# An AdaLN block with attention and a mixture of experts on one core: the eight stores of a sequence's rows to the expert lists are planned one behind the other

## The chip, the cores and the metric

The kernel runs on one core of a Trainium2 chip. The metric is the device time of one execution in microseconds (us). A core has engines that work side by side, each through its own list of instructions in order: TensorE (PE in the profile, its weight loads PEld), VectorE (DVE), ScalarE (ACT), GpSimd (POOL) and SyncE (SP, which here only issues DMA transfers). An engine that has to wait for a semaphore holds up everything behind it in its list.

## The reference, cut to what matters

Eight sequences of 512 tokens with 256 features pass through one transformer block. Its first half is linear attention with a causal running sum, its second half a mixture of eight experts, of which each token uses two:

```python
h = _layernorm(x, axis=-1) * (1 + ca) + sa
x = x + ga * _L0_attn_ref(h, L0_attn_w_qkv, L0_attn_w_out)      # causal linear attention, 16 heads
h = _layernorm(x, axis=-1) * (1 + cb) + sb
x = x + gb * _L0_ffn_ref(h, L0_ffn_router_w, L0_ffn_w1, L0_ffn_w2)

# _L0_ffn_ref, for the tokens xf of all sequences
probs = jax.nn.softmax(xf @ router_w.T, axis=-1)
topv, topi = jax.lax.top_k(probs, 2)
topv = topv / (topv.sum(axis=-1, keepdims=True) + 1e-09)
cw = (jax.nn.one_hot(topi, e, dtype=xf.dtype) * topv[..., None]).sum(axis=1)
h = jax.nn.gelu(jnp.einsum('td,edh->teh', xf, w1), approximate=False)
y = jnp.einsum('teh,ehd->ted', h, w2)
out = jnp.einsum('te,ted->td', cw, y)
```

All of it is float32. The kernel computes only the two chosen experts of each token.

## The kernel before, in words

**Tiling.** A sequence is four chunks of 128 tokens, so there are 32 chunks. For each chunk `early` makes v, q and k (`v_ps`, `qk_ps`), `middle` the denominators and the transposed q and k (`cum_ps`, `qkT_ps`), `late` the scores, the running state and the output product (`s_ps`, `st_ps`, `oT_ps`, `a_ps`), and `rows_of` the second layer norm (`mv_f`, `scaled`, `row`, `rt_ps`).

**Lists of tokens.** After a sequence's fourth chunk, `route` picks two experts per token and a place in each expert's list (`slot`). The lists lie in device memory (`slots`). For each chunk and each of the two choices, POOL issues one indirect DMA that stores 128 rows of 521 numbers (0.27 MB) to their places: eight stores per sequence, 64 in all, line L1015. They are called scatters below. Two scatters of one sequence need not wait for each other: a place belongs to one pair of token and expert.

**Blocks of an expert.** `plan(b, ...)` decides after sequence b which blocks of an expert's list are full. `TAKE` fixes how many: one block of 128 rows after sequence 0, five after sequence 1, three after sequence 2, then two, two, two and four blocks of 256 rows after sequences 3 to 6. What is left is planned after sequence 7 (`plan_rest`, blocks named 8_0, 8_1 and so on). A block is fetched by SP (`fetch`: the weights w1 and w2 of 1 MB each, and the rows `sx` and `r` from the lists), turned by DVE (`xT`), multiplied by w1 and w2 on PE (`h_ps`, `y_ps`) with a Gelu on ACT between (`g`), scaled by DVE (`y`), and added to the result by an indirect DMA from POOL (line L1383). Blocks of sequence b may be read only when all scatters up to those of sequence b have landed.

**The order of the work.** Nothing here is issued as the Python loops run. Each piece of work is noted in a plan (`L.do`, `L.group`, `L.call`) with its engine, an estimate of its time, the tiles that it reads and writes, further works that it has to come behind (`after`), a level and, for a DMA, a landing time and its size. `Plan.run` then walks through time by these estimates: whenever an engine is free it gives it, of the works whose predecessors are done, the one with the lowest level. A DMA counts as done when it has landed: its issue, its `landing`, and its megabytes over a shared channel of 0.26 MB per us. The order that comes out is the fixed order of each engine's list. Attention of sequence b has levels from 4b, a sequence's scatters 4b + 3, expert matmuls 1000 and more, and the other work of blocks -50. So PE prefers attention and takes expert matmuls where no attention is ready. `after` is only an argument of this plan: the semaphores of the program are derived later from the tiles and the DMAs themselves, and `apart` declares that scatters need not wait for each other.

When two indirect DMAs come to stand next to each other on POOL, `give_out` puts a small memset (`between`, line L1519) between them.

Of the kernel before, what the change touches and what calls it, by code (L numbers as in the profile page):

```python
# [339 lines left out]
def kernel(  # L340
# [17 lines left out]
    NC = S // P  # L358
# [42 lines left out]
    scatters = []  # L401
# [532 lines left out]
    def route(q):  # L934
# [79 lines left out]
        def scatter(c, j):  # L1014
            s = nc.gpsimd.indirect_dma_start(  # L1015
                out=slots, out_offset=IndirectOffsetOnAxis(ap=slot.now()[:, c, j : j + 1], axis=0),
                in_=row.now()[:, c, :], in_offset=None,
                bounds_check=NONE - 1, oob_is_err=False,
            )
            apart(s, scattered + cleared, "a slot is of one pair of token and expert")  # L1020
            apart(s, gathered, "blocks that are read are full by then")
            scattered.append(s)
            return s

        L.level += LEVEL["scatter"]
        for c in range(NC):
            for j in range(2):
                scatters.append(
                    L.do(
                        "POOL", 1.29, lambda c=c, j=j: scatter(c, j), r=[slot, row], landing=2.0,  # L1030
                        mb=0.27,
                    )
                )
                scatters[-1].indirect = True
# [435 lines left out]
    for i in range(2):  # L1470
        for t, at in ((acc, TOK), (slots, NONE)):
            L.do(
                "SP", 0.5, lambda t=t, at=at, i=i: clear(t[at + i * P : at + (i + 1) * P, :]),
                after=[modded_], landing=3.0, mb=0.2,
            )
    seqs = {}
    for b in range(B):
        if b not in xs:
            L.level = 4 * b - 12
            load_x(b, after=[X.stores[b - XS]] if b >= XS else ())  # L1480
        L.level = 4 * b + LEVEL["open"]
        q = seqs[b] = open_(b, modded)
        for c in range(NC):
            for part, does in (("early", early), ("middle", middle), ("late", late)):
                L.level = 4 * b + c + LEVEL[part]
                does(q, c)
            L.level = 4 * b + c + LEVEL["rows"]
            rows_of(q, c, modded)

        def store(b=b, q=q):  # L1490
            s = nc.sync.dma_start(
                out=acc[ts(b, S), :].rearrange("(c p) d -> p c d", p=P), in_=q.x.now()
            )
            apart(s, added, "those are of earlier sequences")

        L.level = 4 * b + 3 + LEVEL["route"]
        X.stores.append(L.do("SP", 0.5, store, r=[q.x], landing=3.0, mb=0.5))
        route(q)
        if TAKE[b][0]:
            L.level = 4 * b + 3 + LEVEL["plan"]  # L1500
            blocks = plan(b, list(scatters))
            experts(blocks)
# [76 lines left out]
```

## Time and profile before

| what | us |
|---|---|
| median of 9 runs | 797.13 (794.43 to 798.04) |
| the profiled execution | 796.45 |
| its span from the first to the last instruction | 794.7 |
| PE busy in the span | 755.8 |
| DVE, POOL, ACT busy | 410.8, 319.7, 269.4 |
| the first two scatters start | 89.4 and 91.0 |
| the rows of the first block are fetched from | 111.9 |
| the first matmul of a block starts | 123.9 |
| the last scatter starts | 453.1 |
| the last matmul ends | 786.2 |

The span falls into three stages. Up to about 124 us there is attention only. Up to about 425 us attention and expert blocks share PE. From there to 786 us there are expert blocks only, and then the last sums are added. A group of the profile is named by what it writes and reads, so `h_ps<-xT,w` is the first product of a block. Nearly all operations of the compute engines are issued by one helper and so have line L221. PE's busy time counts a matmul from its start to a modelled end, so it doesn't show how densely the matmuls follow one another. A chunk gives four instructions `qk_ps` and four `a_ps`, and a block of 128 rows 16 `h_ps` and 16 `y_ps`.

### The profile page before, as it was taken

The page shows a single profiled execution, that of the slowest core. Times are in us where ns is not written, and L with a number is a line of the kernel's source. Part 1 is how long each engine was busy: PE and PEld are TensorE (multiplying, and loading weights), DVE is VectorE, ACT ScalarE, POOL GpSimd, SP SyncE. Part 2 cuts the span into 40 slices and gives each one's busy share as a digit, 9 for nine tenths or more (in the row PEclk, how much of TensorE's full clock was granted, in tenths as well). Part 3 has the DMA queues.
Part 4 walks back from the last instruction along what each step waited for, and adds up shares of the span by engine and source line. Part 5 has one row for each costly group of instructions (what it writes and reads, how often), then busy time and mean ns, then how long its engine had stood idle before and what let it go on. Part 6 is the DMA issues. An engine that isn't in the chain of part 4 may idle for free.

```text
span 794.7 us, 16196 instructions
## 1 busy us (share of the span) xinstructions
PE 755.8 (95%) x5824; PEld 620.6 (78%) x5824; DVE 410.8 (52%) x1379; ACT 269.4 (34%) x552; POOL 319.7 (40%) x480
## 2 busy tenths in 40 slices
PE   6799898899999999999999999999999999999995
PEld 2576667667777787778888888888988889888885
DVE  3989998999797866898754610111112111111110
ACT  4555344454634646636413111111111111111110
POOL 5844554726464273373542651312121232120332
PEclk9899999999999999999999999999999999999998
DMA  7322272976865396651666999776886978879961
GB/s 242 99 65 75 86 188 96 310 184 201 200 208 156 109 329 189 190 192 31 203 198 173 293 293 267 205 203 202 239 235 198 286 200 256 219 215 304 273 134 21
DMA packets 132131, 154.30 MB, mean 194 GB/s; under 512 B 43568, under 2 KB 115280, under 8 KB 131920
## 3 DMA queue, kind: packets, MB, share of 16 engines
q1 hardware_dynamic: 116640, 125.24, 52.7%
q0 software_dynamic: 15408, 28.00, 13.9%
q8 instruction: 47, 0.77, 0.4%
q14 instruction: 36, 0.29, 0.1%
HBM read 120.19 MB, written 37.20 MB: 198 GB/s over the span
## 4 chain that ended last, share of the span: by engine, by line
PE 46%; DMA 5%; issue 2%; POOL 1%; SPq 1%; DVE 0%; POOLq 0%
PE h_ps L221 21%; PE y_ps L221 21%; DMA out_dram<-y,to 4%; DMA out_dram<-acc 2%; POOL out_dram L1383 1%; PE oT_ps L221 1%; PE s_ps L221 1%; PE a_ps L221 1%; SPq L1366 1%; PE cum_ps L221 0%; PE rt_ps L221 0%; PE v_ps L221 0%; DVE row L221 0%; PE qk_ps L221 0%; PE qkT_ps L221 0%
## 5 line engine op out<-in xcount | busy, mean ns | idle before, releaser
L221 PE MATMUL h_ps<-xT,w 128*128 128x256 f32 (+1 forms) x1280 | 257.3, 348 | 3.7 <-DVE qk L221 2.7
L221 PE MATMUL y_ps<-w,g 128*128 128x256 f32 x1072 | 253.7, 380 | 0.3 <-issue 0.3
L221 PEld LDWEIGHTS h_ps<-xT,w 128*128 128x128 f32 x1280 | 214.6, 192 | 28.3 <-DVE qk L221 3.1
L221 PEld LDWEIGHTS y_ps<-w,g 128*128 128x128 f32 x1072 | 201.4, 190 | 27.7 <-issue 1.6
L221 ACT ACTIVATE g<-h_ps 128x512 f32<-128x512 f32 x134 | 80.0, 597 | 343.3 <-PE h_ps L221 343.1
L1383 POOL DMA_INDIRECT acc<-y,to x56 | 89.3, 1595 | 221.8 <-DVE y L221 189.5
L221 DVE SCALAR_TENSOR_TENSOR y<-y_ps,cw,r 128x256 f32<-128x256 f32 x67 | 30.0, 480 | 166.9 <-PE y_ps L221 166.8
L221 DVE TENSOR_TENSOR sm<-s_ps,causal 128x512 f32<-128x512 f32 x128 | 82.8, 680 | 9.9 <-PE s_ps L221 9.3
L221 DVE STREAM_TRANSPOSE xT<-sx 128x512 f32<-128x512 f32 (+1 forms) x40 | 24.9, 622 | 121.1 <-PE h_ps L221 69.3
L1015 POOL DMA_INDIRECT slots<-row,slot x64 | 64.6, 1009 | 32.8 <-issue 13.2
L221 POOL TENSOR_TENSOR f<-f,t 128x512 f32<-128x512 f32 x32 | 41.3, 1294 | 59.0 <-DVE t L221 21.0
L221 PE MATMUL qk_ps<-wqkv_sb,hT 128*128 128x512 f32 x128 | 62.2, 612 | 0.0
L221 ACT ACT_TABLE_LOAD x31 | 39.8, 1283 | 4.4 <-DMA cs<-in_cT_dram 3.1
L221 PEld LDWEIGHTS s_ps<-qT,kT 32*128 32x128 f32 x1024 | 32.3, 186 | 11.4 <-issue 8.2
L221 PE MATMUL oT_ps<-sm,vz 128*32 128x128 f32 x1024 | 39.8, 284 | 0.7 <-DVE sm L221 0.5
L1383 POOL DMA_INDIRECT out_dram<-y,to x11 | 17.1, 1555 | 56.4 <-DMA out_dram<-acc 23.1
L221 PE MATMUL s_ps<-qT,kT 32*128 32x128 f32 x1024 | 39.0, 284 | 0.1
L221 PEld LDWEIGHTS qk_ps<-wqkv_sb,hT 128*128 128x128 f32 x128 | 23.7, 195 | 19.0 <-issue 16.9
L221 PE MATMUL v_ps<-wqkv_sb,hT 128*128 128x256 f32 x128 | 35.4, 400 | 3.0 <-DVE t L221 1.9
L221 PE MATMUL a_ps<-wo,oT 128*128 128x256 f32 x128 | 33.5, 384 | 1.0 <-DVE sm L221 1.0
L221 PEld LDWEIGHTS oT_ps<-sm,vz 128*32 128x32 f32 x1024 | 28.6, 113 | 7.4 <-DVE sm L221 1.8
L221 DVE SCALAR_TENSOR_TENSOR row<-scaled,mv_f,mod 128x128 f32<-128x128 f32 x64 | 29.1, 468 | 7.8 <-POOL mv_f L221 6.9
(229 smaller groups left out, 882.3 us busy)
## 6 DMA issues: line engine op xcount, KB each, us to landing
w<-in_w_dram SPq DMA_DIRECT2D x80, 1024.0 KB, 5.8
r<-slots SPq DMA_DIRECT2D x27, 265.0 KB, 5.6
sx<-slots SPq DMA_DIRECT2D x108, 64.0 KB, 6.1
row<-modd SPq DMA_DIRECT2D x8, 512.0 KB, 10.6
acc<-x SPq DMA_DIRECT2D x8, 512.0 KB
out_dram<-acc SPq DMA_DIRECT2D x8, 512.0 KB, 12.3
x<-in_x_dram SPq DMA_DIRECT2D x7, 512.0 KB, 5.1
mod<-modd SPq DMA_DIRECT2D x8, 384.0 KB
```

Source lines behind the costliest of these rows:

```text
L221: return method(now(out), *[now(a) for a in args], **{k: now(a) for k, a in kw.items()})
L1015: s = nc.gpsimd.indirect_dma_start(out=slots, out_offset=IndirectOffsetOnAxis(ap=slot.now()[:, c, j : j + 1], axis=0), in_=row.now()[:, c, ...
L1366: s = nc.sync.dma_start(out=out[b], in_=acc[ts(b, S), :])
L1383: s = nc.gpsimd.indirect_dma_start(out=out.rearrange("b s d -> (b s) d") if block.at_end else acc, out_offset=IndirectOffsetOnAxis(ap=to.n ...
```

## The change

Each scatter of a sequence gets the one ahead of it as a predecessor in the plan. The condition is false for the first scatter of a sequence (the list `scatters` grows by 2 * NC = 8 per sequence), and true for the other seven.

```diff
         L.level += LEVEL["scatter"]
         for c in range(NC):
             for j in range(2):
                 scatters.append(
                     L.do(
                         "POOL", 1.29, lambda c=c, j=j: scatter(c, j), r=[slot, row], landing=2.0,
-                        mb=0.27,
+                        mb=0.27, after=(scatters[-1:][:1] if len(scatters) % (2 * NC) >= 1 else ()),
                     )
                 )
                 scatters[-1].indirect = True
```

In the plan a scatter has landed 1.29 + 2.0 + 0.27 / 0.26 = 4.3 us after its start when the channel is free, and its followers may start 0.25 us later. Without the new argument a sequence's eight scatters are ready together, and since their level is below that of the next sequence they stand in one row on POOL, 1.29 us apart in the plan. With it they stand at least 4.6 us apart in the plan, and POOL's other work is put between them. The instructions themselves, their data and the waits that the program needs for its data are not edited. The order on every engine is computed anew.

## Prediction

> **What bounds the kernel now.** I read the page's busy times and slices first, then busy time by stage, then the waits of PE and DVE in the attention stage, then the timeline around the first expert block.
>
> ```profile
> PE 755.8 (95%) x5824; PEld 620.6 (78%) x5824; DVE 410.8 (52%) x1379; ACT 269.4 (34%) x552; POOL 319.7 (40%) x480
> DVE  3989998999797866898754610111112111111110
> PEclk9899999999999999999999999999999999999998
> ```
>
> PE is busy for 95% of the span, DVE for 52%, but DVE's work lies almost wholly in the first half, where its slices read 9 again and again. The stages (columns: stretch, its length, busy us and instructions of PE, PEld, DVE, ACT, POOL, granted clock, DMA share, GB/s):
>
> ```profile
> 20.00:80.00 60.00, 54.94 (x622) 37.91 (x623) 55.66 (x141) 31.24 (x83) 35.01 (x44) 0.94 0.27 79
> 80.00:120.00 40.00, 35.67 (x407) 24.78 (x406) 38.18 (x120) 15.92 (x40) 23.22 (x35) 0.96 0.53 140
> 120.00:180.00 60.00, 54.13 (x597) 40.37 (x596) 53.89 (x178) 28.63 (x68) 28.27 (x43) 0.97 0.65 194
> 180.00:260.00 80.00, 75.63 (x817) 60.82 (x816) 64.74 (x228) 40.47 (x83) 45.04 (x69) 1.00 0.67 195
> 260.00:420.00 160.00, 157.53 (x1564) 127.66 (x1563) 119.55 (x388) 78.65 (x155) 73.20 (x109) 1.00 0.57 176
> 460.00:780.00 320.00, 320.00 (x1539) 283.48 (x1538) 47.91 (x180) 55.52 (x93) 77.61 (x100) 1.00 0.81 228
> ```
>
> From 20 to 120 us, attention alone, DVE is busy 93.8 of 100 us: there DVE is the bound. From 460 us PE is full and nothing else matters. In between, expert matmuls fill what attention leaves free on PE.
>
> How much PE time is lost per stage has to be counted from work, because busy time includes modelled ends. In the last stage eight rows of 128x256 take 1.73 us, so 0.216 us per 256 columns. A chunk at that rate: v and a 0.87 each, qk 1.73, sums 0.76 on average, the eight transposes 0.87, scores 1.17 and oT 1.08 (32 rows each, as they stand in the timeline), state products 0.57, routing 0.33 (a quarter of a sequence's): 8.3 us. The chunks in a stretch are the mean of its qk_ps and a_ps rows over four; its expert work is twice its y_ps rows times 0.216.
>
> - 20 to 80: 28 and 20 rows, 6 chunks, 49.8 us of work, 10.2 lost, 1.7 per chunk.
> - 80 to 120: 16 and 12 rows, 3.5 chunks, 29.0 of work, 11.0 lost, 3.1 per chunk.
> - 120 to 180: 20 and 21 rows, 5.1 chunks and one block of 128 rows (6.9): 10.8 lost, 2.1 per chunk.
> - 180 to 260: 6 chunks, 56 rows of y_ps (24.2): 6.0 lost, 1.0 per chunk.
> - 260 to 420: 10.5 chunks, 152 rows (65.7): 7.3 lost, 0.7 per chunk.
>
> So losses end where filler is plentiful, and any gain or loss of this change lies before about 430 us. The waits that bear on it (engine, tile, whom it waited for: us, times, longest):
>
> ```profile
> DVE row L221 <- POOL mv_f L221: 6.9, 7, 3.7
> DVE nmr L221 <- POOL mv_a L221: 3.8, 4, 2.1
> PE rt_ps L221 <- DVE row L221: 4.1, 5, 1.1
> ```
>
> POOL, held by eight scatters in a row (8 x 1.29 = 10.3 us), makes DVE wait 10.7 us in the whole run, and PE 4.1 behind that.
>
> ```profile
> 122.66 0.45 DVE L221 STREAM_TRANSPOSE xT<-sx 128x256 f32<-128x256 f32 x1 [3.38 <-DMA sx<-slots]
> 123.92 3.44 PE L221 MATMUL h_ps<-xT,w 128*128 128x128 f32 x16 [2.68 <-DVE qk L221]
> ```
>
> Here DVE stands for 3.4 us at the first block's rows, and PE 2.7 behind it: late rows cost attention too, because DVE works in order.
>
> **The change, part by part.** The 64 scatters stay, at about 0.98 us each. The order of the built program shows where they go. Sequence 0's eight stand behind one another with mv_f, ksum, f, kv and state of sequences 1 to 3 between; the last stands behind sequence 1's first. 27 of the small memsets on POOL vanish (0.09 us each); POOL is 40% busy, so this is worth nothing by itself, and if POOL were the bound it would be 2.4. ACT gets four table loads fewer (31 to 27, at 1.28 us): 5.1 us of ACT, which is half idle in every stage, so nothing.
>
> (A) *The first block comes later.* On PE it stood behind eight finished chunks (a_ps) and stands behind twelve. Four chunks lose their filler. Attention alone lost 10.2 + 11.0 over 9.5 chunks, 2.2 per chunk; the stretch from 120, where these chunks ran, lost 2.1. Four times the difference: +0.4. Bounds by the two attention stretches: 4 x (1.7 - 2.1) = -1.6 and 4 x (3.1 - 2.1) = +4.
>
> (B) *Less filler per chunk afterwards.* Before, 93 us of expert work stood among the last 20 chunks, 4.7 per chunk; now, first block included, 76, so 3.8. The nearest row is 180 to 260, with 24.2 / 6 = 4.0 per chunk, which lost 1.0; the two stretches from 180 together lost 13.3 / 16.5 = 0.8. So 20 x 0.2 = +4. Bounds: the best row (0.7) gives -2, the poorly filled one from 120 (2.1) +26; I take the near row.
>
> (C) *POOL is no longer held for 10 us.* mv_f and mv_a get through between scatters. PE's 4.1 us behind `row` is the visible part; not all of it comes from scatters, so -3. Bounds: 0, and all of DVE's waits, -10.7.
>
> (D) *A new wait.* Sequence 1's seventh and eighth scatter now stand on POOL behind the add of the first block, which waits for its `y`. Behind it stand sequence 2's first scatter, state and f. From `y`: add 1.6, scatter 1.0, scatter 1.0, state 0.75, f 1.3, with gaps 0.8; then 4.3 from the last scatter's issue to landing; then on SP a row load and the slot 0.9, four sx issues 2.4, and 6.1 to landing: 20.1 us. DVE has 64 instructions between that `y` and the xT of block 1_0, 16.5 us at the rows' durations, 17.5 at 94%. DVE is late by 2.6, and PE behind it as in the fence above: +2.6. Bounds: 0, and +7.2 if the sx landing is the 10.7 us from 111.9 to 122.66 there.
>
> The iota that writes the row numbers (L990) now stands soon behind the last scatter of the sequence three before and waits for its landing, some 2 us, five times: 10 us of POOL's idle 60%; taken as 0, at worst the 4.1 us of C again. Rows of block 0_0 have about 30 us of DVE work as cover after sequence 1's `slot`, against some 24 us for the last scatter's landing, 4 MB of weights at the 318 GB/s seen from 140 to 160 us, and the rows: nothing. Sequence 7's last scatter stands behind block 6_0's add, but PE then still has 6_1 to 6_3, 3 x 13.8 = 41 us, against the 20 us chain of D; without them the cost would be up to 20. After that the order is as before, and so is the tail of 8 us behind the last matmul.
>
> Sum: 0.4 + 4 - 3 + 2.6 = +4.0 on the profiled execution's own 796.45 (794.7 of span and 1.8 around it): 800.4. That execution is 0.7 below the median of the runs, so 801.1, rounded to 801.
>
> A side look at the clock: the slices from 80 and 120 us ran at 0.91, and the longest idle pieces of PE in them were 2.3 and 2.7 us. The Trainium skill ("TensorE: Matmul & The Clock Gate", Part 1) lets the clock fall after an idle window of about 3.4 us that runs freely. By that rule D's wait lowers no clock and the sum stays; by the slices it would cost 9% of 20 us once more, 1.8.
>
> **The rivals.** *Smoother POOL wins.* The stretch 120 to 180, where sequence 1's burst (133 to 144 us) and the late first rows both fall, lost 10.8. If spreading frees all of C's 10.7, or most of it beside B's lower bound, and D is hidden, the sum is 0.4 + 0 to -2 - 5 to -10.7: about 790. For it: DVE is the bound there and does wait for mv_f. Against: the first burst ended at 100.1, just when its next input was ready, so it delayed nothing. *Rows come late.* One mechanism: block 1_0's rows, through the POOL add in D. With its upper bound, a stretch at 0.91 and a smaller C, 0.4 + 4 + 7.2 + 1.8 - 1 = +12.4: about 809. It decides if the sx of 1_0 land more than 6 us after DVE reaches xT. Against: DVE too will be slower than its rows. *Nothing measurable.* POOL is idle enough, PE's work is the same, and A to D cancel: 797.
>
> **How the numbers follow.** Forecast (798.7 to 806) 0.45; rows late 0.15; smoother POOL 0.29; nothing 0.11. Within 0.2% (1.6 us) is about what a measurement of this kernel can't tell from no change. So faster 0.29, same 0.11, slower 0.60. The range for 8 in 10 leaves out the far half of smoother POOL and the upper part of late rows: 790 to 811.
>
> **What would show it.** PE's lost time up to 180 us about as before, from 180 to 420 some 4 us more; the first h_ps near 165 us; the waits of DVE on mv_f and mv_a well below 10.7; a wait of DVE xT or PE h_ps of 2 to 4 us at block 1_0; PE full from about 430 us. I am wrong if attention ends earlier with no more loss per chunk (then B is 0 or less), or if PE stands somewhere after 430 us for rows.

## The result, and the profile after

The changed kernel takes 803.77 us (median of 15 runs, 799.37 to 806.33), the kernel before, beside it, 796.48 (45 runs). The ratio is 1.0096, interval 1.0081 to 1.0111: slower by one per cent. Its profiled execution took 802.05 us with a span of 800.3, so 5.6 us above the one of before; the forecast for that difference was 4.0.

The page of the changed kernel (busy times, then DVE and the granted clock in 40 slices):

```profile
PE 754.2 (94%) x5824; PEld 620.4 (78%) x5824; DVE 409.8 (51%) x1379; ACT 265.1 (33%) x548; POOL 319.8 (40%) x453
DVE  4989989899797978887563011111111111111110
PEclk9999899999999999999999999999999999999998
```

The work is the same. The 27 memsets on POOL and the four table loads on ACT are gone as counted, without effect on any end. The stages of the changed kernel (columns as in the prediction):

```profile
20.00:80.00 60.00, 54.95 (x625) 37.91 (x626) 56.63 (x141) 31.13 (x81) 34.28 (x43) 0.97 0.26 79
80.00:120.00 40.00, 33.44 (x372) 24.00 (x371) 36.00 (x115) 15.36 (x38) 19.59 (x24) 0.91 0.36 118
120.00:180.00 60.00, 53.75 (x610) 40.18 (x611) 55.04 (x193) 30.38 (x69) 30.06 (x42) 0.97 0.59 190
180.00:260.00 80.00, 73.82 (x821) 58.57 (x814) 67.68 (x222) 44.57 (x93) 43.54 (x61) 1.00 0.61 182
260.00:420.00 160.00, 157.25 (x1584) 127.37 (x1583) 125.13 (x445) 70.53 (x144) 73.02 (x98) 0.99 0.62 180
460.00:780.00 320.00, 320.00 (x1530) 282.99 (x1529) 49.93 (x186) 55.35 (x93) 79.31 (x102) 1.00 0.82 233
```

Between 80 and 120 us DVE, the bound there, is busy 36.0 us instead of 38.2. From 460 us both kernels are alike.

To see where the time goes I count PE's lost time in slices of 20 us from its rows: the length of a slice less every row at full rate (0.2165 us for 256 columns, 1.1 for 32 score rows, 1.02 for 32 rows of oT, 0.26 for 16 state rows, and so on). Summed up it stands at 44.3 us at 180 us before and at 44.7 after; at 460 us at 57.2 and 61.8. The increase stands mainly in three slices: 180 to 200 (2.7 before, 5.8 after), 260 to 280 (1.2, 4.4) and 420 to 440 (-0.4, 1.6). A row that lies across the edge of a slice is counted in both of its slices, so such sums can be off by about 1 us. If only the part of a row inside the stretch is counted, the loss grows by 1.6 us up to 180 us and by 5.6 us up to 460 us.

The waits of the changed kernel between 20 and 440 us (us, times, longest):

```profile
PE rt_ps L221 <- DVE from_slot L221: 4.6, 1, 4.6
PE rt_ps L221 <- DVE row L221: 3.8, 6, 1.3
DVE xT L221 <- DMA sx<-slots: 7.7, 2, 7.5
DVE row L221 <- POOL mv_f L221: 4.4, 7, 0.9
```

DVE's wait for POOL's mv_f fell from 6.9 to 4.4 us, but PE's wait behind `row` only went from 4.1 to 3.8. The wait for mv_a hardly changed over the whole run, 3.8 us before and 3.5 after: nearly all of it lies in the first 12 us, long ahead of the first store. Here it is in the kernel before between 20 and 440 us, and in the changed kernel over the whole run:

```profile
DVE nmr L221 <- POOL mv_a L221: 0.3, 1, 0.3
```

```profile
DVE nmr L221 <- POOL mv_a L221: 3.5, 3, 2.1
```

So of the 10.7 us that the prediction lays to the rows of stores, 3.5 us have nothing to do with them, and over the whole run the two waits fell from 10.7 to 7.9 us.

Two other waits of the changed kernel stand out, those for `from_slot` and for `sx`. The first, in the timeline of the kernel before and then of the changed one:

```profile
91.78 0.68 PE L221 MATMUL oT_ps<-qT,state 128*128 128x128 f32 x4 [2.26 <-DVE plan_begun L221]
```

```profile
93.49 0.66 PE L221 MATMUL rt_ps<-ident,row 128*128 128x128 f32 x2 [4.62 <-DVE from_slot L221]
```

POOL is free after the first store, so in the plan the next chunk's mv_f, `row` and `rt_ps` go ahead of the oT of the chunk in hand. On the chip DVE has sequence 0's planning to do there, and PE stands 4.6 us instead of 2.3 in front of an `rt_ps` that nothing needed yet. Freeing POOL was not only a gain.

The second wait, 340 us later (timeline of the changed kernel):

```profile
433.45 0.71 DVE L221 STREAM_TRANSPOSE xT<-sx 128x512 f32<-128x512 f32 x1 [7.50 <-DMA sx<-slots]
...
434.35 0.87 DVE L221 SCALAR_TENSOR_TENSOR y<-y_ps,cw,r 128x256 f32<-128x256 f32 x2
...
435.32 1.97 PE L221 MATMUL y_ps<-w,g 128*128 128x256 f32 x8 [1.81 <-issue]
```

These are the rows of block 5_0, stored long before. But SP fetched them only from 426.5 us, having stood 7.3 us for stores of zeros that clear the ends of the lists (L1211). In the new order some of them stand ahead of this fetch. DVE stands 7.5 us in front of the rows, an older block's `y` stands behind that in DVE's order, and PE stands 1.8. The profile names no releaser for PE's wait ("issue"); that `y_ps` had no free buffer is concluded from its start at 435.32, just behind the end of `y` at 435.22.

Last, the clock of the changed kernel, in four stretches of 3.4 us (columns as above; the granted clock is the third number from the end):

```profile
135.10:138.50 3.40, 0.90 (x14) 0.71 (x18) 3.40 (x18) 1.58 (x3) 1.84 (x2) 1.00 0.41 158
138.50:141.90 3.40, 3.40 (x25) 2.02 (x20) 3.40 (x13) 0.00 (x0) 2.01 (x4) 0.53 0.45 101
271.60:275.00 3.40, 1.55 (x11) 1.15 (x10) 3.40 (x13) 0.97 (x2) 0.14 (x1) 1.00 0.39 42
275.00:278.40 3.40, 3.40 (x8) 1.68 (x6) 2.69 (x16) 0.00 (x0) 1.08 (x1) 0.53 0.77 81
```

After a stretch in which PE was busy for 0.90 or 1.55 of 3.4 us, the next runs at about half clock and costs some 1.7 us more. The Trainium skill ("TensorE: Matmul & The Clock Gate", Part 1) has an activity window of 3413 ns that runs freely. The traces agree: the two half-clock pieces here start 136.5 us apart, which is 40 such windows.

### The profile page after: what moved, and what is told of

Its sections match the earlier page's. It is cut to its first block, busy times and chain, and to the rows that moved or that the text cites. A ratio compares the mean times of both kernels' runs of the same rounds, so it can differ in the third digit from the quotient of the medians.

```text
span 800.3 us, 16162 instructions
## 1 busy us (share of the span) xinstructions
PE 754.2 (94%) x5824; PEld 620.4 (78%) x5824; DVE 409.8 (51%) x1379; ACT 265.1 (33%) x548; POOL 319.8 (40%) x453
## 4 chain that ended last, share of the span: by engine, by line
PE 67%; DVE 15%; DMA 8%; POOL 4%; issue 4%; SPq 1%; ACT 1%; POOLq 0%; DVEq 0%; ACTq 0%
PE h_ps L221 25%; PE y_ps L221 24%; PE qk_ps L221 4%; PE oT_ps L221 4%; DMA out_dram<-y,to 3%; DVE sm L221 3%; DVE f L221 3%; PE v_ps L221 2%; PE s_ps L221 2%; PE a_ps L221 2%; DMA out_dram<-acc 2%; DVE den L221 1%; PE cum_ps L221 1%; POOL out_dram L1384 1%; DMA row<-modd 1%
## 5 line engine op out<-in xcount | busy, mean ns | idle before, releaser
L1015 POOL DMA_INDIRECT slots<-row,slot x64 | 67.3, 1052 | 35.9 <-DMA slots<-zeros,plan_ends_i 12.4
L221 PE MATMUL qk_ps<-wqkv_sb,hT 128*128 128x512 f32 x128 | 64.2, 627 | 2.9 <-ACT hT L221 1.6
L1384 POOL DMA_INDIRECT out_dram<-y,to x11 | 17.2, 1560 | 56.4 <-DMA out_dram<-acc 23.2
L221 PE MATMUL oT_ps<-sm,vz 128*32 128x128 f32 x1024 | 37.8, 284 | 0.3 <-DVE sm L221 0.2
L221 ACT COPY oT<-oT_ps 128x256 f32<-128x256 f32 x32 | 11.9, 372 | 71.0 <-PE oT_ps L221 70.9
```

Source lines behind the costliest of these rows:

```text
L221: return method(now(out), *[now(a) for a in args], **{k: now(a) for k, a in kw.items()})
L1015: s = nc.gpsimd.indirect_dma_start(out=slots, out_offset=IndirectOffsetOnAxis(ap=slot.now()[:, c, j : j + 1], axis=0), in_=row.now()[:, c, ...
L1384: s = nc.gpsimd.indirect_dma_start(out=out.rearrange("b s d -> (b s) d") if block.at_end else acc, out_offset=IndirectOffsetOnAxis(ap=to.n ...
```

## The experiments

**What was open.** The forecast's terms say that the loss comes from expert blocks that come later (theory 1). Rival 2: it comes from the new order of POOL's own work. Rival 3: any new order of this program moves its time by about a per cent, either way. The first four kernels were to tell them apart, each written as an edit of the changed kernel. `delay28` has no chain, so POOL stores in rows of eight as before, but a piece of work of 28 us on an engine that does not exist stands in the plan between a sequence's stores and its blocks:

```diff
+    waited = []
...
-                        mb=0.27, after=(scatters[-1:][:1] if len(scatters) % (2 * NC) >= 1 else ()),
+                        mb=0.27, after=(),
...
+        waited.append(L.do("WAIT", 28.0, lambda: None, after=scatters[-2 * NC :]))
...
-            blocks = plan(b, list(scatters))
+            blocks = plan(b, scatters + waited)
```

`chain_first2` and `chain_from2` keep the chain for some of the sequences:

```diff
-    ... if len(scatters) % (2 * NC) >= 1 else ()),
+    ... if len(scatters) % (2 * NC) >= 1 and b < 2 else ()),     (chain_first2)
+    ... if len(scatters) % (2 * NC) >= 1 and b >= 2 else ()),    (chain_from2)
```

`us125`, a control, has no chain and only the estimate of a store changed, from 1.29 to 1.25. In all of them the order is computed anew.

Expected of delay28:

> The scatters are not chained, so they stand in one row on POOL as before. Instead the plan (and only the plan) lets the blocks of a sequence wait 28 us longer after its scatters; the first block then stands behind 13 finished chunks (8 before, 12 in the change). Theory 1, blocks that come later leave PE without filler: ratio 1.007 to 1.013, about the change's 1.0096, with PE's lost time up to 180 us near 45 us and the excess between 180 and 430 us. Rival 2, the cost comes from POOL's order (scatters in the way of attention's POOL work): 0.997 to 1.002. Rival 3, any new order of the lists moves the time by about a per cent either way: no particular value.

Of chain_first2:

> Only the scatters of sequences 0 and 1 are chained, the other six sequences' stand in one row as before. Theory 1: nearly the whole cost is in the stage where blocks are scarce, so 1.005 to 1.010. Rival 2: a quarter of the chained scatters, 1.001 to 1.004. Rival 3: no particular value.

Of chain_from2:

> Only the scatters of sequences 2 to 7 are chained; the first blocks stand where they stood before (behind 8 and 14 chunks). Theory 1: five blocks of sequence 1 are there as filler, so 0.998 to 1.004. Rival 2: three quarters of the chained scatters, 1.005 to 1.009. Rival 3: no particular value.

Of us125:

> A control without any chain: the plan's estimate of a scatter is 1.25 us in place of 1.29. The order changes in many places, the place of the first blocks does not (behind 9 and 14 chunks). Theory 1 and rival 2: 0.998 to 1.002. Rival 3: anything from 0.99 to 1.01, clear of 1.

Measured: delay28 836.28 us, 0.9833 (0.9808 to 0.9858); chain_first2 859.04, 1.0097 (1.0069 to 1.0124); chain_from2 802.81, 0.9436 (0.9408 to 0.9465); us125 851.28, 1.0009 (0.9985 to 1.0034). None of the theories had such numbers, and the reason is the other side of the ratio: the kernel before took 850.29 us here (847.21 to 855.73), 53 more than in all its runs until then.

**Where those 53 us are.** Not spread out. Busy times during four of the eight rows of stores on POOL, first in the profile of us125, whose order is nearly that of the kernel before:

```profile
133.70:143.80 10.10, 7.90 (x62) 5.33 (x60) 6.13 (x33) 1.75 (x5) 8.21 (x15) 1.00 0.54 176
191.00:201.10 10.10, 5.30 (x56) 3.79 (x54) 6.72 (x35) 1.24 (x2) 8.21 (x15) 0.96 0.58 217
304.40:314.50 10.10, 4.36 (x57) 3.41 (x56) 3.97 (x24) 0.86 (x2) 8.14 (x15) 0.92 0.46 177
423.10:433.10 10.00, 4.45 (x49) 3.44 (x48) 4.26 (x32) 0.62 (x2) 8.03 (x15) 0.97 0.77 244
```

And the same rows of stores in the profile of the kernel before that the prediction was made from:

```profile
133.20:143.60 10.40, 10.40 (x113) 7.60 (x115) 10.40 (x45) 3.04 (x8) 8.46 (x15) 1.00 0.56 160
183.00:193.10 10.10, 9.39 (x120) 7.50 (x119) 9.56 (x48) 5.38 (x12) 8.15 (x15) 1.00 0.56 206
342.50:352.70 10.20, 10.20 (x105) 7.94 (x104) 9.93 (x48) 3.42 (x9) 8.31 (x15) 1.00 0.51 192
390.10:400.10 10.00, 10.00 (x104) 8.44 (x103) 6.09 (x33) 2.08 (x5) 7.99 (x15) 1.00 0.68 227
```

POOL does the same in both (15 instructions, 8.0 to 8.5 us, the last busy time of a line). But in us125 PE issues about half as many matmuls meanwhile, and DVE and ACT have less to do. What ACT waited for there can't be named by the profile (timeline of us125):

```profile
314.73 0.37 ACT L221 COPY oT<-oT_ps 128x256 f32<-128x256 f32 x1 [8.66 <-remote]
```

"Remote" means that a semaphore ended the wait and no record tells who raised it. So in this condition PE stands idle for 2 to 6 us within each of these rows (their length less its busy time). In lost time, up to 560 us, us125 has 119.4 us and the kernel before 64.4. Of these 55 us, 34 lie inside the eight rows (43.1 against 9.3) and the rest in the same slices of 20 us: PE's granted clock from 200 to 460 us is 0.93 there, against 1.00. What the chain costs otherwise is buried under that. chain_first2, for one, has two such rows fewer than the kernel before and still takes 9 us more beside it.

**Once more, with the changed kernel beside them.**

> The changed kernel once more, unedited, so that the three others have it beside them on one chip. If the chip is one where ACT and DVE do not stand still without a cause that the profile shows: 1.007 to 1.012 by every theory. If it is one where they do (as in the runs of the first call, where the kernel before took 850 us): the ratio then says nothing of the change, and I expect it anywhere from 0.94 to 1.02.

> The same kernel as delay28 (bursts as before, but the plan lets the expert blocks come some 30 us later). Theory 1 (the time is lost because the expert blocks come later and PE then has less of their work to lay into its gaps): 1.007 to 1.013 to the kernel before, first h_ps near 160 us, and PE's lost time by 460 us 4 to 8 us above that of the kernel before. Rival 2 (the time is lost by the order of Pool's own work): 0.997 to 1.002. Rival 3 (any new order moves the time by up to a per cent either way): anywhere from 0.99 to 1.01.

> The same kernel as chain_first2 (the chain for sequences 0 and 1 alone). Theory 1: 1.005 to 1.010, since the first blocks are already late. Rival 2: 1.001 to 1.004, a quarter of the chained stores. Rival 3: 0.99 to 1.01, with no relation to the other three.

> The same kernel as chain_from2 (the chain for sequences 2 to 7 alone; the first blocks come as early as before). Theory 1: 0.995 to 1.003, and if Pool's freedom (the term of -3 us) holds from there on, the lower half of it. Rival 2: 1.005 to 1.009. In the first call it took 802.8 us with some 15 us in which ACT and DVE stood without a shown cause; without those it would be near 790, which would be 0.992.

Measured, on another chip: after_b 803.51 us, 0.9441 (0.9374 to 0.9507); delay28_b 833.64, 0.9783 (0.9714 to 0.9853); chain_first2_b 857.25, 1.0074 (1.0040 to 1.0109); chain_from2_b 802.52, 0.9431 (0.9364 to 0.9498); the kernel before 851.36. The same condition again, and the same times to 0.4%. The changed kernel, without rows of eight, takes here what it took in the first comparison (803.77), so here it is 5.6% faster than the kernel before.

**One kernel to a comparison.** `chain_half` lets two stores be under way: the predecessor is the one before the last.

```diff
-    after=(scatters[-1:][:1] if len(scatters) % (2 * NC) >= 1 else ()),
+    after=(scatters[-2:][:1] if len(scatters) % (2 * NC) >= 2 else ()),
```

> Each store waits for the one before the last, so that two are under way and a sequence's rows are all stored in about half the time of the full chain. Theory 1 (the expert blocks come later and PE lacks their work): the first block comes between the two kernels, so about half of the loss: 1.003 to 1.006 to a kernel before of 797 us, 798 to 801 us in any case; rival 2 (the order of Pool's work costs): 1.007 to 1.011, as with the full chain; rival 3: 0.99 to 1.01. And of a fourth question, raised by the runs in which the kernel before took 850 us: there PE stood still for 5 to 14 us inside nearly every run of eight and more stores back to back on Pool, and in no run of two or three. If the length of the run is what decides, chain_half (two in a row at most) has none of these standstills before 400 us and takes 798 to 804 us whatever the kernel before takes beside it; if the standstills come from something else, it takes 820 to 855 us where the kernel before takes 850.

Measured: 806.28 us, the kernel before 794.50, ratio 1.0149 (1.0124 to 1.0175). The kernel before is at its usual time again, so the question on the length of a row is not answered by this run. All theories missed: with less chain than the changed kernel it is slower than that. The comparisons from here on had one kernel beside the kernel before, and all found it at 794.5 to 795.6. Whether the chips, of which other ones came up, or the four kernels to a comparison made the condition, was not varied by itself.

So the two kernels that had told most were repeated alone:

> chain_from2 alone with the kernel before beside it (the first two sequences' stores in a row, the others chained). If the kernel before takes about 796 us here, PE is not stopped inside the two rows of stores that are left, and: theory 1 (blocks that come later): 0.995 to 1.003, gaps of PE over 0.7 us between 60 and 440 us adding up to 9 to 13 us (before 12.5, after 18.3); rival 2 (Pool's order): 1.005 to 1.009; rival 3 (every new order of the same work has its own gaps, without a relation to the stores): anywhere from 0.99 to 1.015, with gaps at other places than in either kernel. If the kernel before takes about 850 us: 0.943 once more, by all of them.

> delay28 alone with the kernel before beside it (no chain; Pool's rows of stores as before; the plan holds the expert blocks back by some 28 us). If the kernel before takes about 796 us here: theory 1: 1.007 to 1.013, and gaps of PE over 0.7 us between 60 and 440 us adding up to 17 to 21 us (before 12.5, after 18.3); rival 2: 0.997 to 1.002 with gaps of 11 to 14 us; rival 3: 0.99 to 1.015, whatever the first block's time. If the kernel before takes about 850 us: 0.978 to 0.984 once more, by all of them.

Measured: chain_from2_c 793.57 us against 795.59, 0.9973 (0.9955 to 0.9992); delay28_c 793.66 against 795.20, 0.9982 (0.9962 to 1.0003). The first lies in theory 1's range and contradicts rival 2, and it is the only kernel whose interval lies below 1 where the kernel before takes some 796 us. The second lies in rival 2's range and contradicts theory 1: blocks that come as late as in the changed kernel, or later, cost nothing over the whole run. PE's gaps over 0.7 us between 60 and 440 us say the same: 10.9 us in chain_from2_c, inside theory 1's 9 to 13, and 14.1 in delay28_c, at the upper end of rival 2's 11 to 14 and below theory 1's 17 to 21. So neither theory stands alone, and rival 3 allows both results. And the same row of stores in chain_from2, in the one condition and in the other:

```profile
134.20:144.70 10.50, 6.82 (x59) 5.26 (x58) 6.14 (x33) 1.75 (x5) 8.53 (x15) 1.00 0.55 170
```

```profile
134.50:144.90 10.40, 10.40 (x110) 7.60 (x113) 10.40 (x45) 3.04 (x8) 8.46 (x15) 1.00 0.56 167
```

The program is the same to the last instruction (59 matmuls in chain_from2_b, 110 in chain_from2_c): the standstill belongs to the condition. With two rows of eight left, it costs chain_from2 9 us, against some 55 for the kernel before.

**Which of the first two sequences?** `chain_from1` differs from chain_from2 in sequence 1's stores alone (`b >= 1`).

> The chain for sequences 1 to 7; only sequence 0 stores its rows one behind the other without a wait, so that Pool's and PE's order up to 125 us is the kernel before's. So far: chain from sequence 2 on 0.9973, chain for all 1.0096, blocks merely held back 0.9982. If the loss comes in with sequence 0's chain (Pool, free between its stores, lets the routing steps of the next chunk into DVE's and PE's order ahead of the attention: PE's gap of 4.6 us at 93 us): 0.996 to 1.001, PE's gaps over 0.7 us between 60 and 440 us 10 to 14 us. If it comes in with sequence 1's (its blocks come last in the stretch where DVE is the bound): 1.006 to 1.011, gaps of 16 to 20 us. If every order is its own lot: anywhere from 0.995 to 1.015, with gaps at places that neither the changed kernel nor chain_from2 has. Should the kernel before take about 850 us beside it, the time itself is the measure: 791 to 797 us, or 800 to 804 us plus some 6 us for the one row of stores that is left.

Measured: 807.19 us against 795.38, 1.0159 (1.0134 to 1.0183), slower than the changed kernel, which has sequence 0's chain besides. So between chain_from2 and chain_from1 the loss comes in with sequence 1's chain. But no branch of the expectation holds: the time is above the 1.006 to 1.011 of that branch and a little above rival 3's 1.015, and PE's gaps add up to 12.6 us, as in the kernel before (12.5), where 16 to 20 were expected. Block 1_0's rows come late in fact, as the timeline of chain_from1 shows:

```profile
198.27 0.45 DVE L221 STREAM_TRANSPOSE xT<-sx 128x256 f32<-128x256 f32 x1 [2.20 <-DMA sx<-slots]
198.77 3.00 PE L221 MATMUL h_ps<-xT,w 128*128 128x128 f32 x16 [1.90 <-DVE xT L221]
...
450.23 0.71 DVE L221 STREAM_TRANSPOSE xT<-sx 128x512 f32<-128x512 f32 x1 [13.27 <-DMA sx<-slots]
...
451.80 3.32 PE L221 MATMUL y_ps<-w,g 128*128 128x256 f32 x8 [3.19 <-issue]
```

PE stands 1.9 us for block 1_0's rows, and at the end of attention DVE stands 13.3 us and PE 3.2, as in the changed kernel at 435 us.

**A queue that I had left out.** The waits of SP between 60 and 440 us, in the kernel before, the changed one, and chain_from1:

```profile
SPq L892 <- DMA slots<-row,slot: 1.9, 1, 1.9
```

```profile
SPq L892 <- DMA slots<-row,slot: 14.1, 3, 7.7
SPq L1296 <- DMA slots<-zeros,plan_ends_i: 7.3, 1, 7.3
```

```profile
SPq L892 <- DMA slots<-row,slot: 28.2, 4, 14.3
```

L892 loads a constant part into the buffer `row` of a sequence. There are three such buffers, so SP's load for a sequence waits until the stores of the sequence three before, which read the same buffer, have landed. The weights and rows of blocks stand behind it on SP. With chained stores this wait grows from 1.9 us to 14 and 28. The second line of the changed kernel is the wait of 7.3 us ahead of block 5_0's rows. Such a wait for the clearing stores does not mark the slower kernels by itself: delay28_c has one of 7.8 us between 60 and 440 us, and chain_from2_c, the fastest, the longest of these three:

```profile
SPq L1296 <- DMA slots<-zeros,plan_ends_i: 11.8, 1, 11.8
```

**All of them side by side**, from the profiles of the condition in which the kernel before takes some 796 us. Lost time is counted as above; "expert work" is what h_ps and y_ps rows up to 200 us come to at full rate; "half clock" is half of PE's busy time in the pieces up to 520 us in which the trace has its clock at half, an estimate of what they cost; the last two columns are waits, of DVE from 20 to 460 us and of SP from 60 to 440.

| kernel | ratio | span | lost to 200 us | lost 200 to 520 | half clock | expert work to 200 us | first h_ps | first h_ps of sequence 1 | DVE at sx and r | SP at L892 |
|---|---|---|---|---|---|---|---|---|---|---|
| before | 1 | 794.7 | 47.0 | 8.9 | 5.8 | 16.0 | 124 | 181 | 9.3 | 1.9 |
| chain_from2_c | 0.9973 | 792.7 | 47.3 | 7.4 | 6.5 | 15.2 | 125 | 182 | 8.5 | 2.6 |
| delay28_c | 0.9982 | 795.1 | 55.0 | 1.8 | 11.8 | 6.9 | 176 | 209 | 2.4 | 5.4 |
| changed | 1.0096 | 800.3 | 50.5 | 10.0 | 7.2 | 8.5 | 162 | 198 | 9.7 | 14.1 |
| chain_half | 1.0149 | 804.7 | 52.5 | 12.3 | 13.6 | 10.4 | 132 | 190 | 8.2 | 22.8 |
| chain_from1 | 1.0159 | 804.4 | 51.4 | 15.3 | 9.6 | 7.9 | 123 | 198 | 23.2 | 28.2 |

The sum of the two lost columns differs from that of before by -1.2, +0.9, +4.6, +8.9 and +10.8, the span by -2.0, +0.4, +5.6, +10.0 and +9.7: the count finds the loss to about 1 us, as it must where the work is the same and PE is full from 460 us on. Up to 200 us it goes with the supply, though not step by step: kernels with 15 or 16 us of expert work lose 47, those with 7 to 10 lose 50 to 55. Behind 200 us it does not. delay28 then has the held-back blocks to lay into its gaps, waits for rows least of all (2.4 us), and gets back 7.1 us of the 8.0 it had lost. The kernels that chain sequence 1 get nothing back. The last column has nearly the same order as the lost time: 1.9 to 5.4 us where almost nothing is lost in sum, then 14.1, 22.8 and 28.2.

**The clock's share.** A wait of PE can be paid twice, since half clock can follow it. The stretches of half clock in chain_half that lie behind 100 us, and then those of chain_from1 (columns as above):

```profile
128.90:135.70 6.80, 4.85 (x22) 4.72 (x23) 6.26 (x30) 1.73 (x3) 1.12 (x2) 0.50 0.00 0
183.50:190.30 6.80, 5.76 (x13) 3.21 (x13) 5.46 (x25) 2.44 (x5) 4.43 (x8) 0.50 0.57 144
234.70:238.10 3.40, 3.40 (x21) 3.17 (x23) 3.40 (x14) 1.88 (x3) 1.66 (x2) 0.50 0.81 238
299.60:303.00 3.40, 3.40 (x11) 2.77 (x10) 2.99 (x10) 1.29 (x3) 0.00 (x0) 0.50 0.20 78
```

```profile
175.80:179.20 3.40, 3.24 (x32) 2.63 (x33) 3.40 (x20) 0.61 (x2) 2.48 (x3) 0.50 0.20 78
199.70:203.10 3.40, 3.40 (x21) 3.18 (x23) 3.30 (x14) 0.86 (x2) 0.00 (x0) 0.50 0.43 104
452.30:455.70 3.40, 3.40 (x9) 2.70 (x8) 0.00 (x0) 0.00 (x0) 2.90 (x5) 0.51 0.97 315
```

The last two of chain_from1 come right behind PE's waits of 1.9 and 3.2 us for late rows, shown above. By the table's estimate the clock makes up 7.8 of the 10.0 us by which chain_half's span is longer than that of the kernel before, 3.8 of chain_from1's 9.7 and 1.4 of the changed kernel's 5.6. It does not decide alone: delay28_c has 6.0 us more of it than the kernel before, and its span is only 0.4 us longer.

delay28's own loss sits in one place, where attention is alone for longest; behind it the clock is at half for 10.2 us (timeline of delay28_c):

```profile
127.85 2.08 PE L221 MATMUL a_ps<-wo,oT 128*128 128x256 f32 x4 [4.71 <-DVE sm L221]
```

## Why the prediction was right, and where it was not

The direction, the size's order and most signs held: forecast 801, range 790 to 811, measured 803.8. In steps:

- (A) *The first block comes later*, +0.4. The place held: the first h_ps is at 162.5 us (165 foretold). Lost time at 180 us is up by 0.4 (44.3 to 44.7) by the slices and by 1.6 by the finer count. Both lie in the term's bounds; that one of them is the very number is luck.
- (B) *Less filler per chunk afterwards*, +4. The sum held for this kernel: from 180 to 460 us 17.1 us are lost instead of 12.9, with C's, D's and the clock's part in it. The reason behind it held only in half. Less filler goes with more lost time up to 200 us in the kernels of the table. But delay28 has its blocks later still and is not slower, since filler that is not used early is there later. Lateness by itself is no loss over the run; I priced it as one.
- (C) *POOL is no longer held for 10 us*, -3: the term that failed. DVE's waits on mv_f and mv_a did fall, but only from 10.7 to 7.9 us, as 3.5 us of them come ahead of any store. And PE's wait behind `row` fell by 0.3, not 3, and the freed POOL let routing steps into PE's order ahead of attention, where PE stood 4.6 us instead of 2.3. Chained from sequence 2 on, the kernel loses 1.5 us less behind 200 us (7.4 instead of 8.9), half of the term. But its DVE waits for mv_f for 7.5 us, no less than before (6.9), so this is not shown to be POOL's freedom.
- (D) *A new wait*, +2.6. The chain from late rows over DVE's order to PE is there, but neither at the place nor for the reason I gave. At 1_0 DVE was as slow as its rows (its wait is 0.2 us), as the rival's "against" had it. At 5_0 DVE stood 7.5 us and PE 1.8, since SP waited for clearing stores. For that stretch I had counted on PE's own blocks as cover; but `y` stands behind `xT` on DVE, and PE needs `y`. "PE stands somewhere after 430 us for rows" was my sign of being wrong, and it is there.
- *Left out:* SP's load at L892. I had followed the same buffer's reuse on POOL (the iota at L990, costed at 0) and not on SP. Whether this is what the loss hangs on is not shown, see below.

With what was measured in place of C and D, the sum is 0.4 + 4 - 0.3 + 1.8 = 5.9, against 5.6 between the profiled executions. That is better than the terms deserve. The sum leaves out the 2.3 us by which PE's wait at 93 us grew and the clock's 1.4 us, A and B stand in it as forecast, and B's size is not measured apart from the others. So the direction and the size's order were right with a mechanism that held in part, and that the sum comes so close is luck. The medians lie 7.3 apart, because the changed kernel's profiled execution lay 1.7 us under its median.

The rival "smoother POOL" is not what this kernel does. chain_from2 is 2 us faster than the kernel before, but that POOL's freedom is the reason is not shown. "Rows come late" (809) is about what chain_from1 does (807.2). Costing the clock at nothing was wrong by little: one more half-clock piece, behind the gap at 274 us, some 1.7 us. In chain_half it would be the largest term (7.8 us by the estimate above).

Open: which of the waits makes the loss. The runs narrow it to sequence 1's stores (1.0159 against 0.9973 for that one edit), and delay28 speaks against late blocks as such. SP's wait at L892 has the right order over six kernels, but it was not varied by itself: the test, a fourth buffer for `row`, was not tried. Against it as the only cause: chain_half's DVE waits for rows no longer than the kernel before's (8.2 against 9.3 us), yet it loses 8.9 us, most of it at half clock. Rival 3, that each order has its own lot, would allow nearly all of 0.997 to 1.016, and is not excluded. Open too is what stops the engines during a row of stores, and what sets the condition for it.

## What to carry to other kernels

In a program whose order is planned ahead, a wait written into the plan moves all engines' work around it: five near relatives of one line gave 0.997 to 1.016, so try the variants before explaining one of them. For each buffer whose last reader comes later, look for its next writer, on every queue, and for what stands behind that. Work that fills gaps need not be lost by coming later (delay28); where its data came later than the plan thought, the engine that waited for them stood, and its clock could drop behind that. So count the stretches of half clock in every kernel that is compared. And a change of one per cent that looks settled on one chip can be worth minus six elsewhere: look at the time of the kernel before in every comparison.

## What the runs showed of the hardware

- A row of eight or more indirect stores back to back on POOL passes unnoticed in one condition (PE busy 10.2 of 10.2 us) and holds up PE, DVE and ACT in another (PE busy 4.4 to 7.9 of 10.1 us in the rows above), with POOL itself as fast in both. Stores in twos and threes with other work between did not show it up to 400 us (lost time of after_b from 200 to 400 us: 8.4, of the changed kernel in the first comparison 10.5).
- In the attention stage half clock came in pieces of 3.4, 6.8 or (delay28_c) 10.2 us. A stretch of 3.4 us with PE busy for 1.55 us was idle enough for it; one of 1.58 us, from 432.2 to 435.6 us in the changed kernel, was not followed by it.
- A small DVE instruction is held while POOL runs wide ones, in the changed kernel for example (timeline; start, length):

```profile
180.22 0.76 POOL L221 TENSOR_TENSOR state<-kv,own 128x256 f32<-128x256 f32 x1
180.91 1.28 POOL L221 TENSOR_TENSOR f<-f,t 128x512 f32<-128x512 f32 x1
...
180.26 1.99 DVE L221 TENSOR_TENSOR plan_past<-plan_end,nth 128x24 f32<-128x24 f32 x1
```

`plan_past`, some 0.2 us elsewhere, ends when POOL's second instruction does. The Trainium skill ("SBUF — State Buffer", "SBUF: two separate sides") has a port pair that POOL and a DVE instruction with two SBUF inputs hold in turn, each for its whole instruction; this row agrees. Summed over DVE's instructions between 60 and 440 us, the time above the median of the same instruction is 24.1 us in the kernel before and 19.6 to 22.4 us in the five others of the table, so it explains none of the loss.
